# A fixed order for ScalarE's copies, turns and squares in a linear-attention layer on one Trainium2 core

## The chip, the cores and the metric

The kernel runs on one core of a Trainium2 chip. A core has five engines that work side by side and wait for each other by semaphores: TensorE (PE, matrix products into PSUM banks), VectorE (DVE, elementwise work), ScalarE (ACT, functions of one input, with a table for each kind), GpSimd (POOL) and SyncE (SP), of which the last two mostly issue DMA transfers here. The metric is the device time of one execution in microseconds; of several executions the median counts. Before the change it is 1413.25 us, the median of 3 runs (1410.88 to 1413.98).

## The reference

One input `x` of 2048 tokens by 512 channels; 16 heads of 128 channels, 4 lags. Cut to what matters:

```python
xn = layernorm(x)
q, k, v = [conv4(silu(xn @ W)) for W in (Wq, Wk, Wv)]   # causal, per channel
z, a, b = xn @ Wz, xn @ Wa, xn @ Wb
q, k = rotary(q), rotary(k)
q, k = q / max(|q|, 1e-12), k / max(|k|, 1e-12)          # per head
out = 0
for s in range(4):                                        # lag of s tokens
    attn = einsum('bshd,bshd->bsh', q, lag(k, s)) / sqrt(128)
    out += (attn * sigmoid(lag(a, s) * b))[..., None] * lag(v, s)
out = out * rsqrt(mean(out * out) + 1e-6) * norm_w * silu(z)
s = out @ Wout
g = silu((relu(xn @ sign(up).T * up_scale) @ sign(down).T) * down_scale)
return x + s * g
```

All in f32. The square of `out` (called o in the kernel) is only used for the mean over all 2048 channels, which the kernel applies at the very end, so o's squares can be added up beside the rest. The lengths of q and k don't change under the rotation, so the squares of q and k before it serve for the norms.

## The kernel before

The tokens go in 4 blocks of 512 (b = 0 to 3), the heads in 8 pairs (p = 0 to 7). A tile of a pair is 128 partitions by 2 halves by 512 tokens; each half (j = 0, 1) comes from its own PSUM bank.

`step(p, b)` is the unit. It computes q and k of pair p for block b+1, and v, z, the weighted sum o and the output projection of pair p for block b. So a stage b = -1 computes only q and k of block 0 (beside the sign network `ups`/`downs` of block 0, which fills PE), stages b = 0 to 2 do both, and a last loop does v, z and the output for block 3. The sign networks of blocks 1 to 3 follow as a tail of matmuls.

For each of q, k and v the path is the same. `project` multiplies on PE (4 matmuls a half) and ACT evicts the bank with a Silu into a "raw" tile (L330). The raw tile has 3 edge columns ahead of its 512, filled by `with_halo` (L291) from what `keep_halo` (L296) saved from the block before; after the Silus, its own last 3 columns are saved. `convolve` then takes the first product on ACT (L342, a multiplication by one weight for each half) and the three further taps for each half on DVE. The raw tiles of q and k share two buffers in turn: the raw q of the next step lies where the raw q of this step was.

k and v themselves also need edge columns, since lagged copies of them are read; they are copied by the same two helpers. `k`, `v` and `q` have one buffer each: the copy of edge columns into the next `k` waits until DVE has read the last one in its products, the one into `v` until DVE has formed the weighted terms `te`.

`turn(q)` makes the rotated copies of q: a multiplication of both halves on ACT (L371), then four operations on DVE. `products` squares q and k on ACT (L403, L404: `sq0` and `sq1`, two squares each), adds the two by a DMA (L405), multiplies q by the lagged k on DVE (`pr`) and sums `pr` by head on PE (`dots`). At the change of blocks (p = 0) the norms of q and k are taken (`norms`, a square root on ACT), inverted on DVE (`norms_in_rows`, which also saves `kept_r` on ACT, L490) and made into coefficients, which go through DRAM (`co_dram`) and come back broadcast (`bc`).

`weighted` multiplies the lagged v by `bc` on DVE into two tiles `te`, adds them to o, squares o on ACT (L554) into a spare tile and adds it to `o2_dram` by a DMA that POOL issues (in the profile `o_dram<-te` in stage 0, `o_dram<-xnT` later). In stage 0 that spare tile is the second `te`. `gated_output` makes `oz` of o, the norm's weight and z on DVE. After each odd p, `output_projection` multiplies `oz` of two pairs by the output weights (`po`), ACT copies the bank (L590) and a DMA adds it in DRAM.

Two wrappers `pe` and `dve` keep TensorE's and VectorE's instructions in the order of the program text. What goes through `nc.scalar` is placed by the scheduler; a third wrapper `act` keeps the order of the few ScalarE instructions given to it. Instructions of the same engine run in the order in which they were placed, each after its own waits, so an instruction that waits holds up all behind it. Most lines that go through a wrapper show as L76 in the profile.

Of the kernel before, what the change touches and what calls it, by code (L numbers as in the profile page):

```python
# [38 lines left out]
F32 = mybir.dt.float32  # L39
F32R = mybir.dt.float32r  # L40
AF = mybir.ActivationFunctionType
ALU = mybir.AluOpType
PSUM = bass.MemoryType.PSUM

P = 128
# [5 lines left out]
HALO = LAGS - 1  # L51
# [3 lines left out]
TB = 512  # L55
NTB = S // TB
# [25 lines left out]
def recurrent_layer(ctx: ExitStack, tc: tile.TileContext, a: dict, out: bass.AP):  # L82
# [204 lines left out]
    def with_halo(pool, name, tag, bufs, p, b):  # L287

        t = pool.tile([P, 2, HALO + TB], F32, tag=tag, name=f"{name}_{p}_{b}", bufs=bufs)

        (act if name in ("rv", "v") and p == b == 0 else nc.scalar).copy(t[:, :, 0:HALO], kept[name][:, p])  # L291
        return t

    def keep_halo(name, t, p, b):
        if b < NTB - 1:
            nc.scalar.copy(kept[name][:, p], t[:, :, TB : TB + HALO])  # L296

    def first_product(to, second_half):

# [68 lines left out]
    def turn(q):  # L368

        q0, q1 = q[:, LAGS - 1], q[:, LAGS - 2]  # L370
        nc.scalar.mul(q1, q0, turns[:, 0:1])  # L371
        for j in range(2):
            dve.scalar_tensor_tensor(
                q1[:, j, :], q0[:, 1 - j, :], turns[:, 2 - j : 3 - j], q1[:, j, :], ALU.mult, ALU.add
            )

        for s in range(2, LAGS):
            at = LAGS - 1 - s
            dve.scalar_tensor_tensor(
                q[:, at], q[:, at + 1], turns[:, 3:4], q[:, at + 2], ALU.mult, ALU.subtract  # L380
            )

    def products(p, b, q, between=None, beside_k=None):

        n = f"_{p}_{b}"
        if p or b:
            load(qks, "k", p, b)
        q0 = q[:, LAGS - 1]
        k = with_halo(qks, "k", "k", 1, p, b)
        raw = raw_of(qks, "k", p, b)  # L390
        if p == 0:
            sum_squares(p)
        convolve(1, p, raw, k[:, :, HALO:])
        keep_halo("k", k, p, b)
        if between:
            between()
        turn(q)
        if beside_k:
            beside_k()

        sq = [qks.tile([P, 2, TB], F32, tag=f"sq{j}", name=f"sq{j}" + n, bufs=3 - 2 * j) for j in range(2)]
        for j in range(2):
            nc.scalar.activation(sq[j][:, 0], q0[:, j], AF.Square)  # L403
            nc.scalar.activation(sq[j][:, 1], k[:, j, HALO:], AF.Square)  # L404
        nc.gpsimd.dma_start(sq[0], sq[1], accum_op=ALU.add)  # L405
        squares_due.append((p, sq[0]))
        def product(to, j, lo, hi):

            k0 = k[:, j, lo : lo + TB]
            k_lags = bass.AP(k0.tensor, k0.offset, [k0.ap[0], [1, hi - lo], k0.ap[1]])  # L410
            dve.tensor_tensor(to, q[:, lo:hi, j, :], k_lags, ALU.mult)

        pr = qks.tile([P, LAGS, TB], F32, tag="pr", name="pr0" + n, bufs=2)
        product(pr, 0, 0, LAGS)
        if not b or p % 2 == 0:
            pr1 = qks.tile([P, LAGS, TB], F32, tag="pr", name="pr1" + n, bufs=2)
            product(pr1, 1, 0, LAGS)
            if b:
                nc.gpsimd.dma_start(pr, pr1, accum_op=ALU.add)
            elif p < NP - 1:  # L420
                dve.tensor_tensor(pr, pr, pr1, ALU.add)
        else:

            product(q[:, :, 1], 1, 0, LAGS)
            dve.tensor_tensor(pr, pr, q[:, :, 1], ALU.add)
        if not b:

            prs = [pr, pr1] if p == NP - 1 else [pr]
            dots_due.append([p, prs, of_head[:, p], p == NP - 1, True])
            return  # L430


        for h in range(0, P, D // 2):
            first, second = slice(h, h + D // 4), slice(h + D // 4, h + D // 2)
            if p % 2 == 0:
                nc.gpsimd.dma_start(pr[first], pr[second], accum_op=ALU.add)
            else:
                both = dots_due[-1][1][0]
                nc.gpsimd.dma_start(both[second], pr[first])
                nc.gpsimd.dma_start(both[second], pr[second], accum_op=ALU.add)  # L440
        if p % 2 == 0:
            dots_due.append([p, [pr], of_heads[:, p // 2], p == NP - 2, False])
        else:
            dots_due[-1][-1] = True
# [61 lines left out]
        nc.sync.dma_start(co_dram[b].rearrange("s r t -> (s r) t"), rk)  # L506

    gated = {}

    def values(p, b, raw):  # L510

        v = with_halo(vs, "v", "v", 1, p, b)
        convolve(2, p, raw, v[:, :, HALO:])
        keep_halo("v", v, p, b)
        return v

    wos = {}
# [12 lines left out]
    def weighted(p, b, v):  # L530

        n = f"_{p}_{b}"
        parts = []
        for lo in range(0, LAGS, 2):

            bc = vs.tile([P, 2, TB], F32, tag="bc", name=f"bc{lo}" + n, bufs=3)
            for h in range(2):
                row = co_dram[b][lo : lo + 2, 2 * p + h, :]
                sp.dma_start(
                    bc[h * D // 2 : (h + 1) * D // 2], row.partition_broadcast(D // 2)  # L540
                )

            v0 = v[:, :, lo : lo + TB]
            v_lags = bass.AP(v0.tensor, v0.offset, [v0.ap[0], [1, 2], *v0.ap[1:]])
            te = vs.tile([P, 2, 2, TB], F32, tag=f"te{lo}", name=f"te{lo}" + n, bufs=1)
            dve.tensor_tensor(te, v_lags, bc.unsqueeze(2).to_broadcast([P, 2, 2, TB]), ALU.mult)
            parts.append(te)
        dve.tensor_tensor(parts[0], parts[0], parts[1], ALU.add)
        o = parts[0][:, 0]
        dve.tensor_tensor(o, o, parts[0][:, 1], ALU.add)  # L550


        o2 = xnT[:, p % 2 * 2 : p % 2 * 2 + 2, HALO : HALO + TB] if b else parts[1][:, 0]
        nc.scalar.activation(o2, o, AF.Square)  # L554
        if p == 0:
            pool.dma_start(o2_dram[b], o2)
        else:
            pool.dma_start(o2_dram[b], o2, accum_op=ALU.add)
        return o

    def gated_output(p, b, o, z):
# [58 lines left out]
    def step(p, b, beside_q=None, beside_k=None):  # L620

        at = b >= 0
        change = p == 0 and at
        q = queries(p, b + 1)
        rv = with_halo(vs, "rv", "raw", 1, p, b) if p == b == 0 else None
        if beside_q:
            beside_q()
        if change and b:
            sum_squares(p)
            norms(b)  # L630
        due = bool(dots_due) and dots_due[0][-1]
        if change and not b:

            def beside_k():
                norms(b)
                norms_in_rows(b)

        products(p, b + 1, q, (lambda: norms_in_rows(b)) if change and b else None, beside_k)
        if z_due:
            z_due.pop()()  # L640
        if at:
            load(vs, "v", p, b)
            raw = raw_of(vs, "v", p, b, 1, rv)
        if first_due:
            first_due.pop()()
        if at:
            v = values(p, b, raw)

        def strips():

            if p and p % 2 == 0:
                sum_squares(p)
            if p == NP - 2 and b + 2 < NTB:
                gate_products(b + 2)
            if p == 1 and not at:
                gate_products(0)
            if due:
                sum_dots()


        output_projections(strips if p % 2 == 0 or due else None)
        if change:
            coefficients(b)
        if at:
            load(vs, "z", p, b)
            load_wo(p, b)
            z = []
            z_of = lambda: z.append(gates_of_output(p, b))
            out_of = lambda: gated_output(p, b, weighted(p, b, v), z[0])
            if change:  # L670
                z_due.append(z_of)
                first_due.append(out_of)
            else:
                z_of()
                out_of()
        if p == (3 if at else 2):
            load_gate(b + 1)
        elif p == (4 if at else 3):
            gate()
        if b + 2 < NTB:  # L680
            if p < TC:
                statistics(b + 2, p)
            if p == TC - 1:
                centre(b + 2)
            elif p == 5:
                divide(b + 2)
# [138 lines left out]
    loads["by"] = sp  # L825
    load(vs, "v", 0, last)
    raw = raw_of(vs, "v", 0, last, 1)
    load(vs, "v", 1, last)
    load(vs, "z", 0, last)
    sum_squares(None)  # L830
# [31 lines left out]
    for p in range(NP + 1):  # L862
# [3 lines left out]
        if p:  # L866
            weights["z"] = z_weights.pop(p - 1)
            z = gates_of_output(p - 1, last)

        if p % 2 == 1 and p != 3 or p == 4:  # L870
            output_projections()
# [245 lines left out]
```

## Time and profile before

| what | value |
|---|---|
| median of 3 runs | 1413.25 us |
| the profiled execution's own time | 1409.21 us |
| its span, first to last instruction | 1407.4 us |
| mean granted TensorE clock | 0.997 |
| DVE's wait `te` on the broadcast coefficients | 16.8 us in 4 waits, longest 12.5 |
| ACT's wait for DVE before the edge columns of v (L291) | 112.1 us in 31 waits |
| ACT's wait for DVE before keeping v's columns (L296) | 78.6 us in 24 waits |
| ACT's wait for DVE before o's square (L554, `xnT`) | 58.2 us in 24 waits |
| ACT's wait for DVE before q's first square (L403) | 39.1 us in 27 waits |
| issue to landing of the DMAs of o's square | 3.8 to 13.4 us, median 8.1 |

A wait is the idle time of an engine just before an instruction, with the engine and instruction whose end released it. It costs time only where the waiting engine is the one that sets the end, or where something that this engine needs stands behind it. "L76 DVE k <- ACT k L342" reads: DVE's operation that writes k stood idle until ACT's line 342 had written k.

The busy share of each engine by stretch (start and end in us, busy time and number of instructions of PE, PEld, DVE, ACT, POOL, then granted clock, DMA share, GB/s):

```profile
0.00:200.00 200.00, 198.17 (x671) 110.10 (x672) 180.08 (x205) 127.70 (x254) 47.94 (x81) 1.00 0.79 223
200.00:340.00 140.00, 136.69 (x347) 58.42 (x346) 133.80 (x132) 66.49 (x139) 18.23 (x25) 1.00 0.81 207
340.00:630.00 290.00, 290.00 (x727) 125.03 (x726) 271.81 (x266) 133.61 (x273) 55.23 (x69) 1.00 0.86 198
630.00:860.00 230.00, 227.96 (x578) 97.46 (x577) 214.71 (x209) 105.79 (x212) 45.77 (x56) 0.99 0.81 190
860.00:1060.00 200.00, 197.97 (x494) 84.90 (x493) 182.23 (x171) 83.57 (x159) 35.25 (x43) 1.00 0.76 171
1060.00:1250.00 190.00, 189.53 (x500) 92.55 (x499) 124.89 (x116) 54.23 (x95) 34.21 (x44) 1.00 0.90 231
1250.00:1407.00 157.00, 150.79 (x653) 122.31 (x651) 84.89 (x135) 38.84 (x59) 0.00 (x0) 0.99 0.22 68
```

Stage b = -1 ends near 215 us, the stages 0, 1 and 2 near 500, 775 and 1052, the last loop near 1230.

### The profile page before, as it was taken

Reading aid. Unit: us, or ns where it says so; the run is one execution under the profiler, and the core shown is the slowest. Engines: PE = TensorE matmul, PEld = TensorE weight load, DVE = VectorE, ACT = ScalarE, POOL = GpSimd, SP = SyncE. Lnnn points to the kernel's source line nnn. Section 1 sums busy time; section 2 is a strip of 40 time slices with the busy share of each in tenths; the row PEclk is TensorE's granted clock in tenths of the full one; section 3 lists DMA queues with packets and bytes.
Section 4 is the critical chain, followed back from the end, with each engine's and each line's share of the span. In section 5 each row is a group of like instructions: output and inputs, shape, how many; then the busy total and the mean of one; then the engine's idle time right before and its main releaser. Section 6 shows DMA issues by size and latency. Waiting matters only on the chain. (4 is left out here: it accounts for less than half of the span.)

```text
span 1407.4 us, 12413 instructions
## 1 busy us (share of the span) xinstructions
PE 1391.1 (99%) x3962; PEld 690.8 (49%) x3962; DVE 1192.4 (85%) x1231; ACT 610.2 (43%) x1189; POOL 236.6 (17%) x317
## 2 busy tenths in 40 slices
PE   9999999999999999999999999999999999999998
PEld 6555544344444444444444444444434444578886
DVE  7998989999998999998999999898985997247454
ACT  7667655445444443354434533444432333232122
POOL 2222111111213121112231112020201122200000
PEclk9999999999999999999999999999999999999999
DMA  9977577889989588888977797887858989863020
GB/s 314 338 195 176 133 200 180 223 204 189 212 202 210 141 194 222 209 197 196 219 161 181 170 250 182 194 199 169 170 100 187 262 243 215 169 221 115 25 90 31
DMA packets 104985, 263.40 MB, mean 187 GB/s; under 512 B 17812, under 2 KB 18324, under 8 KB 100568
## 3 DMA queue, kind: packets, MB, share of 16 engines
q0 software_dynamic: 36672, 108.02, 39.6%
q1 hardware_dynamic: 68248, 154.58, 35.9%
q8 instruction: 32, 0.52, 0.1%
q14 instruction: 33, 0.27, 0.1%
HBM read 159.77 MB, written 52.45 MB: 151 GB/s over the span
## 5 line engine op out<-in xcount | busy, mean ns | idle before, releaser
L76 PE MATMUL po<-wo,oz 128*128 128x512 f32 x512 | 228.3, 599 | 7.4 <-DVE oz L76 7.4
L76 PE MATMUL pq<-xnT,wq 128*128 128x512 f32 (+1 forms) x528 | 226.2, 580 | 0.2 <-ACT xnT L76 0.2
L76 PE MATMUL pz<-xnT,wz 128*128 128x512 f32 x512 | 225.2, 592 | 0.5 <-ACT rv L330 0.5
L76 PE MATMUL pk<-xnT,wk 128*128 128x512 f32 x512 | 225.2, 592 | 0.0
L76 PE MATMUL pv<-xnT,wv 128*128 128x512 f32 x512 | 225.2, 592 | 0.0
L76 DVE SCALAR_TENSOR_TENSOR k<-rk,conv_w,k 128x512 f32<-128x512 f32 x192 | 142.3, 751 | 25.2 <-ACT k L342 20.6
L76 PEld LDWEIGHTS po<-wo,oz 128*128 128x128 f32 x512 | 96.5, 191 | 136.3 <-issue 109.1
L76 DVE SCALAR_TENSOR_TENSOR q<-rq,conv_w,q 128x512 f32<-128x512 f32 x192 | 141.5, 749 | 23.0 <-ACT q L342 16.2
L76 DVE TENSOR_TENSOR te<-v,bc 128x2048 f32<-128x2048 f32 x64 | 144.0, 2288 | 18.9 <-DMA bc<-co_dram 16.8
L76 PEld LDWEIGHTS pq<-xnT,wq 128*128 128x128 f32 x528 | 99.0, 189 | 123.1 <-issue 112.0
L76 PEld LDWEIGHTS pz<-xnT,wz 128*128 128x128 f32 x512 | 96.6, 189 | 124.2 <-issue 118.7
L76 PEld LDWEIGHTS pv<-xnT,wv 128*128 128x128 f32 x512 | 96.6, 189 | 123.7 <-issue 118.5
L76 PEld LDWEIGHTS pk<-xnT,wk 128*128 128x128 f32 x512 | 96.6, 189 | 120.5 <-issue 117.4
L76 DVE SCALAR_TENSOR_TENSOR v<-rv,conv_w,v 128x512 f32<-128x512 f32 x192 | 141.3, 750 | 6.9 <-ACT v L342 2.4
L76 DVE SCALAR_TENSOR_TENSOR q<-q,turns 128x1024 f32<-128x1024 f32 (+1 forms) x128 | 127.1, 1013 | 2.3
L76 DVE TENSOR_TENSOR pr<-q,k 128x2048 f32<-128x2048 f32 x52 | 117.3, 2287 | 0.9
L76 DVE CAST hid_hi<-hid 128x512 fp32r<-128x512 f32 x52 | 22.2, 427 | 92.3 <-ACT hid L732 92.3
L732 ACT ACTIVATE hid<-ph,up_scale 128x512 f32<-128x512 f32 x64 | 43.8, 685 | 109.0 <-PE ph L76 108.1
L76 PE MATMUL ph<-xs_hi,up 128*128 128x512 f32 x192 | 76.9, 400 | 0.1
L76 PE MATMUL ph<-xs_lo,up 128*128 128x512 f32 x192 | 75.7, 394 | 0.0
L76 DVE TENSOR_TENSOR te<-te,te 128x2048 f32<-128x2048 f32 x32 | 73.3, 2292 | 1.1
L405 POOL DMA_DIRECT2D sq<-sq x32 | 34.3, 1072 | 201.6 <-ACT sq L404 119.3
(148 smaller groups left out, 1678.0 us busy)
## 6 DMA issues: line engine op xcount, KB each, us to landing
bc<-co_dram SPq DMA_DIRECT2D x128, 256.0 KB
pr<-pr POOLq DMA_DIRECT2D x72, 256.0 KB, 5.7
wq<-in_wq_dram SPq DMA_DIRECT2D x32, 512.0 KB
wk<-in_wk_dram SPq DMA_DIRECT2D x32, 512.0 KB
sq<-sq POOLq DMA_DIRECT2D x32, 512.0 KB, 6.5
wv<-in_wv_dram SPq DMA_DIRECT2D x32, 512.0 KB
wz<-in_wz_dram SPq DMA_DIRECT2D x32, 512.0 KB
wo<-in_wo_dram SPq DMA_DIRECT2D x32, 512.0 KB
```

Source lines behind the costliest of these rows:

```text
L76: return self.tc.keep_in_program_order(getattr(self.engine, op)(*args, **kwargs))
L405: nc.gpsimd.dma_start(sq[0], sq[1], accum_op=ALU.add)
L732: nc.scalar.activation(hid, ph, AF.Relu, scale=scale)
```

## The change

Four things move in ScalarE's order, and all the moved instructions now go through `act`:

- The edge columns of k and v. `sum_with_halo` takes the place of `with_halo` and `keep_halo` for these two: the last columns of a tile are saved only when the next tile of the same name is made, which is after the Silus of its raw input, and the edge columns are filled then too.
- q's turn goes through `act`, in its old place in the text: behind k's convolution.
- The squares of q and k, and their DMA, come straight behind the turn, ahead of `beside_k`.
- o's square and its DMA are put into a list, `o_due`, and issued behind the next step's q (`queries`), or, in the last loop, behind the Silus of the next z.

```diff
--- before.py
+++ after.py
@@ -288,12 +288,26 @@
 
         t = pool.tile([P, 2, HALO + TB], F32, tag=tag, name=f"{name}_{p}_{b}", bufs=bufs)
 
-        (act if name in ("rv", "v") and p == b == 0 else nc.scalar).copy(t[:, :, 0:HALO], kept[name][:, p])
+        (act if name == "rv" and p == b == 0 else nc.scalar).copy(t[:, :, 0:HALO], kept[name][:, p])
         return t
 
     def keep_halo(name, t, p, b):
         if b < NTB - 1:
             nc.scalar.copy(kept[name][:, p], t[:, :, TB : TB + HALO])
+
+
+
+    to_keep = {}
+
+    def sum_with_halo(pool, name, p, b):
+
+        if name in to_keep:
+            to_keep.pop(name)()
+        t = pool.tile([P, 2, HALO + TB], F32, tag=name, name=f"{name}_{p}_{b}", bufs=1)
+        act.copy(t[:, :, 0:HALO], kept[name][:, p])
+        if b < NTB - 1:
+            to_keep[name] = lambda: act.copy(kept[name][:, p], t[:, :, TB : TB + HALO])
+        return t
 
     def first_product(to, second_half):
 
@@ -368,7 +382,7 @@
     def turn(q):
 
         q0, q1 = q[:, LAGS - 1], q[:, LAGS - 2]
-        nc.scalar.mul(q1, q0, turns[:, 0:1])
+        act.mul(q1, q0, turns[:, 0:1])
         for j in range(2):
             dve.scalar_tensor_tensor(
                 q1[:, j, :], q0[:, 1 - j, :], turns[:, 2 - j : 3 - j], q1[:, j, :], ALU.mult, ALU.add
@@ -386,24 +400,24 @@
         if p or b:
             load(qks, "k", p, b)
         q0 = q[:, LAGS - 1]
-        k = with_halo(qks, "k", "k", 1, p, b)
         raw = raw_of(qks, "k", p, b)
         if p == 0:
             sum_squares(p)
+        k = sum_with_halo(qks, "k", p, b)
         convolve(1, p, raw, k[:, :, HALO:])
-        keep_halo("k", k, p, b)
         if between:
             between()
         turn(q)
+
+        sq = [qks.tile([P, 2, TB], F32, tag=f"sq{j}", name=f"sq{j}" + n, bufs=3 - 2 * j) for j in range(2)]
+        for j in range(2):
+            act.activation(sq[j][:, 0], q0[:, j], AF.Square)
+            act.activation(sq[j][:, 1], k[:, j, HALO:], AF.Square)
+        nc.gpsimd.dma_start(sq[0], sq[1], accum_op=ALU.add)
+        squares_due.append((p, sq[0]))
         if beside_k:
             beside_k()
 
-        sq = [qks.tile([P, 2, TB], F32, tag=f"sq{j}", name=f"sq{j}" + n, bufs=3 - 2 * j) for j in range(2)]
-        for j in range(2):
-            nc.scalar.activation(sq[j][:, 0], q0[:, j], AF.Square)
-            nc.scalar.activation(sq[j][:, 1], k[:, j, HALO:], AF.Square)
-        nc.gpsimd.dma_start(sq[0], sq[1], accum_op=ALU.add)
-        squares_due.append((p, sq[0]))
         def product(to, j, lo, hi):
 
             k0 = k[:, j, lo : lo + TB]
@@ -506,12 +520,16 @@
         nc.sync.dma_start(co_dram[b].rearrange("s r t -> (s r) t"), rk)
 
     gated = {}
+    o_due = []
+
+    def squares_of_o():
+        while o_due:
+            o_due.pop(0)()
 
     def values(p, b, raw):
 
-        v = with_halo(vs, "v", "v", 1, p, b)
+        v = sum_with_halo(vs, "v", p, b)
         convolve(2, p, raw, v[:, :, HALO:])
-        keep_halo("v", v, p, b)
         return v
 
     wos = {}
@@ -551,11 +569,15 @@
 
 
         o2 = xnT[:, p % 2 * 2 : p % 2 * 2 + 2, HALO : HALO + TB] if b else parts[1][:, 0]
-        nc.scalar.activation(o2, o, AF.Square)
-        if p == 0:
-            pool.dma_start(o2_dram[b], o2)
-        else:
-            pool.dma_start(o2_dram[b], o2, accum_op=ALU.add)
+
+        def square():
+            act.activation(o2, o, AF.Square)
+            if p == 0:
+                pool.dma_start(o2_dram[b], o2)
+            else:
+                pool.dma_start(o2_dram[b], o2, accum_op=ALU.add)
+
+        o_due.append(square)
         return o
 
     def gated_output(p, b, o, z):
@@ -622,6 +644,7 @@
         at = b >= 0
         change = p == 0 and at
         q = queries(p, b + 1)
+        squares_of_o()
         rv = with_halo(vs, "rv", "raw", 1, p, b) if p == b == 0 else None
         if beside_q:
             beside_q()
@@ -825,6 +848,7 @@
     loads["by"] = sp
     load(vs, "v", 0, last)
     raw = raw_of(vs, "v", 0, last, 1)
+    squares_of_o()
     load(vs, "v", 1, last)
     load(vs, "z", 0, last)
     sum_squares(None)
@@ -866,6 +890,7 @@
         if p:
             weights["z"] = z_weights.pop(p - 1)
             z = gates_of_output(p - 1, last)
+        squares_of_o()
 
         if p % 2 == 1 and p != 3 or p == 4:
             output_projections()
```

The compiled program has the same instructions on PE and DVE in the same order as before. On ScalarE the order differs, on POOL the DMAs of o's squares come later among the others.

## The prediction

> **What bounds the kernel now.** I read the busy times first, then what TensorE (PE) waited for, then VectorE's (DVE) and ScalarE's (ACT) waits, then the timeline around each PE wait.
>
> ```profile
> PE 1391.1 (99%) x3962; PEld 690.8 (49%) x3962; DVE 1192.4 (85%) x1231; ACT 610.2 (43%) x1189; POOL 236.6 (17%) x317
> ```
>
> PE is busy for all but 16.3 of 1407.4 us. An edit of ACT's order adds and removes no matmul, so it can win only PE's waits (and the slower matmuls that follow one), and lose by new waits. These are PE's waits, with total, times and longest:
>
> ```profile
> PE po L76 <- DVE oz L76: 7.4, 3, 3.3
> PE unread L76 <- DVE still L690: 1.6, 1, 1.6
> PE pz L76 <- ACT rv L330: 0.5, 1, 0.5
> ```
>
> The three waits for oz (the gated output) are the prize. The timeline puts them at 275.07 (3.31 us, stage b=0), 845.62 (2.04, b=2) and 1056.13 (2.02, start of the last stage). The rest of the idle time is the start (1.6 + 0.2) and a tail of some 6 us after the last matmul, which holds no moved instruction. The second wait costs more than its length:
>
> ```profile
> 275.07 5.42 PE L76 MATMUL po<-wo,oz 128*128 128x512 f32 x12 [3.31 <-DVE oz L76]
> ...
> 845.62 7.11 PE L76 MATMUL po<-wo,oz 128*128 128x512 f32 x12 [2.04 <-DVE oz L76]
> ```
>
> The same twelve matmuls take 5.42 us after the first wait and 7.11 after the second: 1.7 us more, and in the stretch 845.62 to 849.50 the granted clock was 0.68 of full against 1.00 after the first wait. So the second wait is worth 2.04 + 1.7 = 3.7 us.
>
> oz comes from DVE, which in stages b=0 to 2 has little air: in the windows 340 to 630 and 630 to 860 us it is busy 272 of 290 and 215 of 230. What it waits for there is ACT:
>
> ```profile
> DVE k L76 <- ACT k L342: 20.6, 16, 1.8
> ...
> DVE q L76 <- ACT q L342: 16.2, 12, 3.6
> ```
>
> ACT is only 43% busy, so these are questions of order. Line 342 is the first multiplication of a convolution, on which DVE's three taps for each half wait. Just before the wait of 845.62, DVE and then ACT:
>
> ```profile
> 800.79 4.56 DVE L76 SCALAR_TENSOR_TENSOR q<-rq,conv_w,q 128x512 f32<-128x512 f32 x6
> 807.17 4.57 DVE L76 SCALAR_TENSOR_TENSOR k<-rk,conv_w,k 128x512 f32<-128x512 f32 x6 [1.83 <-ACT k L342]
> ```
>
> ```profile
> 805.38 1.15 ACT L371 ACTIVATE q<-q,turns 128x1024 f32<-128x1024 f32 x1 [1.12 <-DVE q L76]
> 806.43 0.71 ACT L342 ACTIVATE k<-rk,conv_w 128x512 f32<-128x512 f32 x1
> ```
>
> q's turn (L371) needs q complete, and k's first multiplication, whose input is ready at 804.3, stands behind it: DVE idles 1.83 = 1.15 + 0.71 less an overlap. From there to 845.62 DVE runs almost without a gap.
>
> **The change part by part.** Nothing is added or removed; PE's and DVE's orders are the same, ACT's changes.
>
> *Turn and squares behind k's first products.* At p=1 of b=2 the compiled order now has k's first multiplication straight behind the first Silu of raw k: the 1.83 goes to 0. In most odd steps, though, another thing stands there: the copy of the next raw q's edge columns (0.1 to 0.2) waits for DVE to end q's convolution, since the two raw slots take turns, and it lies ahead of the second Silu of raw k (0.58), behind which the kept columns (3 x 0.1) and the multiplication (0.65 to 0.71) now follow. DVE then idles 0.1 + 0.6 + 0.3 + 0.7 = about 1.8 where it idled 1.83 (p=3 of b=1, at 598.40: no change). Where the copy lies behind that Silu (p=1 of b=1, at 519.76) it is 1.2: 0.6 won.
>
> *Step p=5 of b=1.* Before, the gate's sigmoid and its two table loads (1.28 + 0.63 + 1.28) stood ahead of q's second multiplication: idle of 2.75 at 668.23 and 0.83 at 673.63. Now they stand behind both; the 1.8 of the last paragraph takes their place: 2.75 + 0.83 - 1.8 = 1.8 earlier (2.0 with the 0.25 at 663.16). *Step p=7 of b=1*: 0.84 + 1.41 + 1.41, part of it behind o's square (1.06), becomes 1.8: 1.9 earlier. *p=0 of b=2*: the copy of the norms' last columns, which waits for DVE's reciprocal, now stands ahead of q's turn: DVE waits 1.15 + 0.2 = 1.4; in return an idle of 0.46 at 771.40 goes. In sum DVE reaches the oz of 845.62 earlier by 2.0 + 1.9 - 1.4 + 0.5 + 1.8 = 4.8 us, and 2.04 was wanted: that wait goes, with its slow matmuls: **-3.7**. Bounds: 0 (none of the idle is won) to -3.7.
>
> *Last steps of b=2.* DVE's idle before the wait of 1056.13:
>
> ```profile
> 1019.46 2.33 DVE L76 SCALAR_TENSOR_TENSOR q<-rq,conv_w,q 128x512 f32<-128x512 f32 x3 [0.85 <-ACT q L342]
> 1023.09 2.33 DVE L76 SCALAR_TENSOR_TENSOR q<-rq,conv_w,q 128x512 f32<-128x512 f32 x3 [1.31 <-ACT q L342]
> 1027.25 4.57 DVE L76 SCALAR_TENSOR_TENSOR k<-rk,conv_w,k 128x512 f32<-128x512 f32 x6 [1.83 <-ACT k L342]
> ```
>
> All three go: o's square stands behind q's multiplications, the turn behind k's. 4.0 won where 2.02 is wanted: **-2.0** (bounds 0 to -2.0). The wait of 0.48 on ACT at 1111 is covered then: **-0.5**.
>
> *Edge columns of k and v kept later.* ACT waited 78.6 us for DVE's v to keep its columns and 112.1 for the v buffer, with the Silus of z and the eviction of po behind it. PE lost only the 0.48 by that, so the gain on PE is inside the sums above.
>
> *First stage (b=-1).* Its steps p=1, 2, 3, 7 also get the copy ahead of k's multiplications, where before k's first product ran early: DVE's k comes 1.2 to 2.3 us later. PE there waits for DVE's split of the hidden layer, with 0.6 to 4.4 us to spare at its four uses; at the use near 129 us, 0.63 is to spare and about 1.0 is taken: **+0.3** (bounds 0 to +1.7, the whole lateness).
>
> *o's square behind the next q, at p=0 of b=0.* The square ran at 259.29 and its DMA was issued at 260.64, landing 7.6 us later, and the second product of the next weighted sum (268.28, which waited 0.72 for that landing) writes the same buffer. Now the square stands behind the first Silu of raw k (input at 259.6): issue about 1.0 later, so the first PE wait grows: **+0.9**, beside the 0.3 of before (bounds 0 to +1.7).
>
> *o's squares in the last stage.* The last one moves from 1201 behind the Silu of z (input 1208.2), its DMA from 1204.1 to 1210, landing some 8.6 later; then the load and sum of squares, done at about 1224.7 against 1219. The RMS rows are wanted at some 1230 by PE, whose chain behind them waited 0.13 at 1252.98: **+0.3** (bounds 0 and +3, with the longest landing of these DMAs, 13.4, in place of 8.6).
>
> **Sum**: -3.7 - 2.0 - 0.5 + 0.3 + 0.9 + 0.3 = -4.7. The profiled execution took 1409.2 (span 1407.4, 1.8 around it), so it would take 1404.5. It lies 4.0 below the median of 1413.25; the runs spread from 1410.9 to 1414.0. On the median: **1408.5 us**.
>
> [...]
>
> **The rivals.**
> *R1, half clock after the first wait.* That wait grows to 4.2 us. Price, by the rows of twelve matmuls: 7.11 - 5.42 = 1.7. For: 2.04 was enough at 845. Against: 3.31 was not at 275. 1404.5 + 1.7, on the median 1410.2.
> *R2, the second gain is not won.* DVE's gains of p=5 and p=7 are taken back at the block change, where the norms' rows go through DMAs (DVE waited 16.8 us in 4 for such rows, once 12.5): then DVE comes only 1.8 - 1.4 + 0.5 = 0.9 earlier at 845.62, the wait shrinks to 1.1 with its slow matmuls. -4.7 + 1.1 + 1.7 = -1.9: 1411.3. Against: before the wait at 845.62 no such DMA wait stands.
> *R3, the moved instructions don't matter.* PE waited on ACT for 0.7 us in all; what DVE wins goes into other idle time: within 1 us of 1413.
> *R4, slower: the edge copy of the next raw q becomes DVE's bound.* Place: the odd steps of b=1, where each first tap of k comes 1.8 us after q's last. If ACT's queue gives none of the old idle back (its Silus of raw k come no earlier, as the gate's table loads still stand ahead of them), p=5 and p=7 pay 1.8 each. The output projections there have 0.53 (699.04) and 1.39 us (771.83) to spare, so it decides from a loss of 0.5 in p=5. The waits up to 845.62 then grow by 3.6, and with the +1.2 of the first stages the time is +4.8, nothing else won: 1418.0. For: the copy is ahead in ten steps, and margins are thin. Against: the 1.8 stands where 3.6 and 3.7 us of idle stood.
>
> **How the numbers follow.** Forecast 0.47, R1 0.13, R2 0.12, R3 0.08, R4 0.20. A measurement of this kernel tells some 0.2% (2.8 us) from no change. The forecast (-4.7) counts as faster, R1 (-3.0) for half faster and half no change, R2 and R3 as no change, R4 as slower. Faster 0.54, same 0.26, slower 0.20. Low end: all 7.4 of the waits for oz, 0.5 and 1.7 won with none of the losses is -9.6, which is 1403.6 on the median; the end is set just inside it, at 1404.0. High end: near R4, 1417.5. The likeliest one's own range is 1405 to 1411.
>
> **What would show it.** Right: PE's waits for oz are one, near 275, of 4 to 4.5 us; the twelve matmuls at 845 take 5.4; DVE's wait for q's multiplication falls from 16.2 to under 8; k's stays near 20. The first stage: a wait of about 0.3 near 129. Wrong: waits for oz at 699 or 772 (R4), or one left near 845 (R2); a granted clock under 1 behind the first wait (R1). The forecast also falls if ACT's copies or Silus become PE's releasers, which would mean that a PSUM bank comes free too late.

## The result, and the profile after

The changed kernel takes 1408.65 us, the median of 11 runs (1407.85 to 1413.32), where the kernel before took 1413.07 beside it (11 runs, 1410.2 to 1413.98). The ratio on record is 0.9984, with a 95% interval of 0.9976 to 0.9992: 2.2 us faster, between 1.1 and 3.4, which is half of the 4.4 us between the medians. The forecast was 1408.5. In a later series, 12 runs of the changed kernel (median 1410.56) against 29 of the one before (1411.19) gave 0.9995 [0.9984, 1.0006]. So the change is worth between nothing and some 3 us, and the agreement of the median says less than it seems to: the profiled executions below tell which of the forecast's steps held.

The profiled execution after took 1410.8 us, span 1408.9. What TensorE waited for in it (total, times, longest):

```profile
PE po L76 <- DVE oz L76: 6.2, 1, 6.2
PE unread L76 <- DVE still L713: 1.6, 1, 1.6
PE ph L76 <- ACT hid L755: 1.6, 1, 1.6
PE pz L76 <- ACT rv L344: 1.1, 1, 1.1
PE pf L76 <- DVE hid_lo L76: 0.9, 1, 0.9
```

The three waits for oz have become one. The waits near 845 and 1056 us are gone, but the first is 6.2 us where it was 3.3, and there are two new waits (pf, ph) and a longer one (pz). The timeline of TensorE at the one that is left, and of VectorE just ahead of it:

```profile
278.96 7.39 PE L76 MATMUL po<-wo,oz 128*128 128x512 f32 x12 [6.17 <-DVE oz L76]
```

```profile
266.81 2.29 DVE L76 TENSOR_TENSOR te<-v,bc 128x2048 f32<-128x2048 f32 x1
272.18 2.29 DVE L76 TENSOR_TENSOR te<-v,bc 128x2048 f32<-128x2048 f32 x1 [3.07 <-DMA o_dram<-te]
```

The twelve matmuls take 7.39 us, not 5.42: half clock now follows the first wait (the granted clock is 0.50 from 276.15 to 282.98 us, and single matmuls of po take up to 1220 ns where 592 is the median). VectorE stood 3.07 us for the landing of o's first square, 0.72 before the change. The places where time is lost, by profile (the slower matmuls are those twelve less 5.42; the second profile is that of `changed_again`, below):

| us | before | after | after, second profile | four_mended (below) |
|---|---|---|---|---|
| hidden layer's split, near 131 | 0 | 0.88 | 0.89 | 0 |
| first oz wait, near 275 | 3.31 | 6.17 | 4.61 | 2.51 |
| slower matmuls behind it | 0 | 1.97 | 2.98 | 0 |
| second oz wait and slower matmuls, near 845 | 3.73 | 0 | 0 | 0 |
| third oz wait, near 1056 | 2.02 | 0 | 0 | 0 |
| raw v, near 1097 | 0.47 | 1.07 | 1.36 | 0 |
| behind the RMS root, near 1254 | 0.13 | 1.58 | 2.03 | 1.93 |
| sum | 9.7 | 11.7 | 11.9 | 4.4 |
| the profiled execution's own time | 1409.21 | 1410.8 | 1412.84 | 1402.43 |

The sums follow the times, but in the second profile only in part: its time is 3.6 us over the one before, its sum 2.2. What the rest went into the table doesn't hold; the mean granted clock of that execution was 0.995, that of the two ahead of it in the table 0.997. The profiled executions of the changed kernel lie 2 us above its medians, the one of the kernel before some 4 below its median, so they show the places and not the verdict.

What the change was to bring, VectorE at p=1 of b=2, it brings: k's convolution follows q's without a gap, where 1.83 us stood.

```profile
804.04 4.56 DVE L76 SCALAR_TENSOR_TENSOR q<-rq,conv_w,q 128x512 f32<-128x512 f32 x6
808.51 4.56 DVE L76 SCALAR_TENSOR_TENSOR k<-rk,conv_w,k 128x512 f32<-128x512 f32 x6
```

VectorE's waits after (total, times, longest) show one line that the profile before did not have, the second:

```profile
DVE k L76 <- ACT k L356: 23.2, 16, 2.3
DVE te L76 <- ACT v L76: 16.4, 3, 12.6
...
DVE q L76 <- ACT q L356: 8.7, 5, 3.4
```

The weighted sum waits for ScalarE's copy of v's edge columns, once for 12.6 us. That is in the last stage, and matters below.

### The profile page after: what moved, and what is told of

It reads as the page before. It is cut to its first block, busy times and chain, and to the rows that moved or that the text cites. A ratio compares the mean times of both kernels' runs of the same rounds, so it can differ in the third digit from the quotient of the medians.

```text
span 1408.9 us, 12420 instructions
## 1 busy us (share of the span) xinstructions
PE 1390.8 (99%) x3962; PEld 690.6 (49%) x3962; DVE 1191.8 (85%) x1231; ACT 612.4 (43%) x1189; POOL 236.1 (17%) x317
## 4 chain that ended last, share of the span: by engine, by line
PE 83%; DVE 8%; DMA 5%; issue 1%; ACT 1%; SPq 1%; POOL 0%; DVEq 0%; ACTq 0%; POOLq 0%
PE pq L76 14%; PE pk L76 14%; PE po L76 14%; PE pz L76 13%; PE pv L76 12%; PE pf L76 7%; PE ph L76 7%; DVE te L76 2%; DVE q L76 2%; DVE k L76 1%; PE dots L76 1%; DVE v L76 1%; PE squares L76 1%; DMA y<-s_dram 1%; DMA bc<-co_dram 1%
## 5 line engine op out<-in xcount | busy, mean ns | idle before, releaser
L76 DVE SCALAR_TENSOR_TENSOR k<-rk,conv_w,k 128x512 f32<-128x512 f32 x192 | 141.7, 751 | 27.7 <-ACT k L356 23.2
L344 ACT ACTIVATE rq<-pq 128x512 f32<-128x512 f32 x62 | 37.0, 596 | 109.8 <-PE pq L76 109.6
```

What stands on the lines that cost most here:

```text
L76: return self.tc.keep_in_program_order(getattr(self.engine, op)(*args, **kwargs))
L344: nc.scalar.activation(to[:, j, :], pp, AF.Silu)
```

## The experiments

All times are medians, ratios are against the kernel before, measured in the same series of runs. The changed kernel has two ratios, 0.9984 and 0.9995, and its median differs by 1.9 us between its two series, while the expectations mostly count from the first one, 1408.65. So a time is best compared by its ratio. A "margin" is the time from the end of VectorE's first piece of a pair's oz, on which the waits above fell, to the start of the matmul that reads it, worked out from the trace, where TensorE did not wait.

**The next raw q's edge copy behind the squares** (`rq_edge_behind`). The tile is made right behind the squares, pinned there, and handed to the next step:

```diff
+        next_rq.append(with_halo(qks, "rq", "raw", 2, (p + 1) % NP, b + (p + 1) // NP))
...
-        convolve(0, p, raw_of(qks, "q", p, b), q0)
+        convolve(0, p, raw_of(qks, "q", p, b, raw=next_rq.pop() if next_rq else None), q0)
```

> The changed kernel with one thing moved: the copy of the next raw q's edge columns goes behind this step's squares of q and k, so it no longer stands ahead of k's first multiplications. Theory A (the changed kernel's k is late in the odd steps because ScalarE waits in that copy for VectorE to end q's convolution): VectorE's wait for k's multiplication falls from 23.2 us in 16 to under 12; the wait of 0.88 us at 131 us goes; the weighted sum of the first stage starts about 1.5 us earlier and the first oz wait shrinks from 6.2 us to 3 to 5; the oz margins before the old waits near 847 and 1054 grow from 2.0 and 2.2 us to over 3. Time 1 to 4 us under the changed kernel's 1408.65: 1404.5 to 1407.5. Rival B (the size of the first wait is set by when the DMA of o's first square lands, whatever VectorE does before): the first wait stays at 5 to 6.5 us, time within 1 us of 1408.65.

Measured: 1411.12 us (12 runs), 0.9993 [0.9982, 1.0003]. VectorE does come earlier: the margins near 562, 704 and 847 us grow from 1.1, 2.5 and 2.0 to 2.6, 5.2 and 3.2. But the one near 1053 stays at 2.20, and the ratio lies between those of the changed kernel. Nothing waited at these places any more. VectorE's wait for k does not fall either (24.6 us): in the step p=7, where it now waits 3.9, VectorE has caught up with TensorE, and waits for raw k itself. The wait at 131 us stays at 0.88, so there the copy isn't the cause; A falls for the first stage. The first oz wait is 4.4 us with a landing wait of 1.3 in it, which tells little, as the changed kernel's second profile has 4.6 and 1.5.

**A tile of its own for o's squares in stage 0** (`own_tile_for_square`).

```diff
-        o2 = xnT[:, p % 2 * 2 : p % 2 * 2 + 2, HALO : HALO + TB] if b else parts[1][:, 0]
+        o2 = xnT[:, p % 2 * 2 : p % 2 * 2 + 2, HALO : HALO + TB] if b else vs.tile([P, 2, TB], F32, tag="o2", name="o2" + n, bufs=1)
...
-        oz = vs.tile([P, 2, TB], F32, tag="oz", name=f"oz_{p}_{b}", bufs=3)
+        oz = vs.tile([P, 2, TB], F32, tag="oz", name=f"oz_{p}_{b}", bufs=2)
```

> The changed kernel with o's squares of stage 0 in a tile of their own (room is made by two buffers of oz in place of three), so that no product of the weighted sum waits for a DMA to land. Theory A (of the first oz wait of 6.2 us, 3.1 are the wait for the DMA of o's square and the rest is VectorE's lateness): the 3.07 us wait of VectorE for that DMA is gone, the first oz wait is 3.0 to 3.5 us, the time 2.5 to 5 us under 1408.65 (the slower matmuls behind the wait may go too). Rival B (two buffers of oz or another transfer take its place): the wait stays over 5 us, or new waits for oz appear; time within 1 us of 1408.65 or above.

Measured: 1407.96 us (12 runs), 0.9971 [0.9959, 0.9983]. The landing wait is gone and the first oz wait is 2.99 us, as A said; slower matmuls still follow it (the twelve take 7.11 us). The median is only 0.7 us under 1408.65; by the ratios the gain is 1.8 to 3.4 us, near A's lower end. The wait for raw v grew to 1.9 us and takes part of it back. The edit also takes one of oz's three buffers away. VectorE shows it at 1198.50, where oz waits 9.2 us for TensorE's output projection, but in time that it would else spend on v's edge copy, for which 0.9 us of waiting is left (more on that copy below).

**The turn and the squares free again, the rest changed** (`turn_and_squares_old`).

```diff
-        act.mul(q1, q0, turns[:, 0:1])
+        nc.scalar.mul(q1, q0, turns[:, 0:1])
...
-            act.activation(sq[j][:, 0], q0[:, j], AF.Square)
+            nc.scalar.activation(sq[j][:, 0], q0[:, j], AF.Square)
```

The squares also stand behind `beside_k` again.

> The changed kernel with q's turn and the squares of q and k back as before the change (free for the scheduler, squares behind what runs beside k); the edge columns and o's squares stay changed. Theory A (the waits near 845 and 1056 went because k's first products no longer stand behind the turn): VectorE's wait for k's multiplication rises from 23 us to over 28 with 1.8 us each at the odd steps of stage 2; the oz margins at 847 and 1054 fall from 2.0 and 2.2 us to under 1, with one of the two waits back at 0.2 to 2 us; time 1409 to 1413. Rival B (it is o's square behind q's multiplications that brought the gain): both waits stay away and the time is within 1 us of 1408.65.

Measured: 1429.81 us (4 runs), 1.0122 [1.0104, 1.014]; far beyond both theories. ScalarE at p=1 of b=1, and VectorE there:

```profile
533.00 1.15 ACT L385 ACTIVATE q<-q,turns 128x1024 f32<-128x1024 f32 x1 [1.61 <-DVE q L76]
534.05 0.58 ACT L344 ACTIVATE rk<-pk 128x512 f32<-128x512 f32 x1
...
535.47 1.33 ACT L356 ACTIVATE k<-rk,conv_w 128x512 f32<-128x512 f32 x2
```

```profile
536.22 4.56 DVE L76 SCALAR_TENSOR_TENSOR k<-rk,conv_w,k 128x512 f32<-128x512 f32 x6 [3.25 <-ACT k L356]
```

With the edge columns kept late, both of k's first products stand behind the second Silu of raw k. If the turn is free, the scheduler puts it ahead of that Silu, and k waits for turn, Silu, copies and product: 3.25 us where the kernel before had 1.83. VectorE's wait for k is 39.3 us in all (23.2 after), and oz is waited for five times, 14.7 us. The run takes back the turn and the squares together; that the turn is what costs is read from the trace.

**The edge columns as before, the rest changed** (`edge_columns_old`). `with_halo` and `keep_halo` are back for k and v.

```diff
-        k = sum_with_halo(qks, "k", p, b)
         convolve(1, p, raw, k[:, :, HALO:])
+        keep_halo("k", k, p, b)
```

> The changed kernel with the edge columns of k and v filled and kept as before the change; turn, squares and o's squares stay changed. Theory A (keeping the columns late costs in the first stage, since k's first product can no longer run ahead of the second Silu, and wins nothing on TensorE later): the wait of 0.88 us at 131 us goes, the first oz wait shrinks by 1 to 2 us, no wait near 845 or 1054; ScalarE's waits for VectorE before v's edge columns and before keeping them are back at some 100 and 70 us. Time 1405.5 to 1408. Rival B (late keeping is what frees ScalarE for the Silus and q's first products): waits for oz near 845 or 1054 come back with 1 to 2 us each; time 1410 to 1413.

Measured: 1426.74 us (4 runs), 1.0107 [1.0087, 1.0126]. Again far beyond both. VectorE's wait for k does fall, to 6.1 us, but a wait for the turn takes its place: 33.1 us in 25. ScalarE and then VectorE at p=0 of b=0:

```profile
250.56 0.20 ACT L296 COPY kept_k<-k 128x6 f32<-128x6 f32 x1 [1.57 <-DVE k L76]
250.66 1.14 ACT L76 ACTIVATE q<-q,turns 128x1024 f32<-128x1024 f32 x1
```

```profile
251.84 2.73 DVE L76 SCALAR_TENSOR_TENSOR q<-q,turns 128x512 f32<-128x512 f32 x3 [1.31 <-ACT q L76]
```

The pinned turn stands behind the instruction that was written just ahead of it on ScalarE, and with the old helper that is the copy that keeps k's last columns, which waits for VectorE to end k. So VectorE ends k, and must wait a copy and a multiplication for the turn: 1.31 us, nearly every step. The two parts of the change lean on each other: late columns need the turn behind k's products, and a pinned turn needs the columns kept late. On this reading neither has a price of its own.

**o's squares at once, the rest changed** (`o_squares_old`): `square()` in place of `o_due.append(square)`, through `nc.scalar`.

> The changed kernel with all of o's squares issued at once and free for the scheduler, as before the change; turn, squares of q and k and edge columns stay changed. Theory A (the place of o's squares gives part of the gain in the stages and part of the loss in the last one): VectorE's first products of q wait behind the square at some steps or not, the oz margins at 847 and 1054 stay over 1 us; the wait for raw v at 1097 is 0.5 or less; time 0 to 1.5 us under the changed kernel of the same call. Rival B (like the other two parts, taken back alone it costs much): new oz waits of over 3 us in all, time over 1415.

Measured: 1411.77 us (12 runs), 1.0 [0.999, 1.0011], 1.2 us over the changed kernel of the same series (1410.56), which is within what can be told. VectorE comes a little later (the margin near 847 is 0.6 in place of 2.0), the wait for raw v is gone, and the one behind the RMS root is 3.0 us. This part alone moves little.

**The last stage's squares as before** (`last_squares_old`), and **only the sign weights' loads put behind the squares** (`up_load_behind_square`).

```diff
-        o_due.append(square)
+        square() if b == NTB - 1 else o_due.append(square)
```

```diff
-            pool.dma_start(up[:, some], signs_dram["up"][:, some])
+            o_due.append(lambda: pool.dma_start(up[:, some], signs_dram["up"][:, some]))
```

> The changed kernel with o's squares of the last stage alone as before the change (at once, free for the scheduler, their DMAs ahead of the sign weights' loads on GpSimd's queue). Theory A (the late squares cost at two places of the last stage: the first load of sign weights, no longer held behind o's DMA, runs ahead of the broadcast coefficients near 1078 us, and the last square holds the output's DMAs on GpSimd's queue near 1212 to 1224 us): TensorE's wait for raw v (1.07 us at 1097) falls to 0.5 or less, though the 2 us gained ahead of it stay; the wait for the hidden layer behind the RMS root (1.58 us at 1254) falls to 0.5 or less. Time 1406 to 1407.5, that is 1 to 2.5 us under the changed kernel's 1408.65. Rival B (both waits are DMA latency that differs from run to run): they stay within 0.5 us of 1.07 and 1.58, time within 1 us of 1408.65.

> The changed kernel with the loads of the sign weights in the last stage put behind o's squares, as their order on GpSimd's queue was before the change; the squares stay late. Theory A: the broadcast of the coefficients lands before 1083 us, VectorE's wait for it falls from 15.4 us to 13 to 14, the wait for raw v at 1097 goes to 0.5 or less; the wait behind the RMS root stays at 1 to 2.9 us. Time 0.5 to 1.5 us under 1408.65. Rival B (the load doesn't matter, the broadcast lands when other transfers let it): wait of 15 us or more, wait for raw v still 1 us or more.

Measured: 1409.96 us (0.9993 [0.9982, 1.0004]) and 1409.61 us (0.9991 [0.9981, 1.0001]), 12 runs each. In both the wait for raw v is gone, and VectorE's wait for the broadcast coefficients is 13.0 and 12.0 us (15.4 after): in the changed kernel GpSimd sends 512 KB of sign weights at 1077.67, in the middle of these broadcasts, because the square whose DMA had stood ahead of that load now comes later. That part of A is shown, by the loads alone too, and all fourteen profiles agree: where the load runs ahead (eight) that wait's longest is 15.3 to 17.1 us and raw v is waited for 1.1 to 1.9, where it does not (six) 11.9 to 13.2 and 0 to 0.6. But the wait behind the RMS root grew to 2.3 and 4.7 us, so A falls there, and the time gained at raw v is paid again.

**The first stage as before** (`first_stage_old`): for block 0 of q and k, `with_halo`, `keep_halo`, the free turn and the free squares.

```diff
+        k = with_halo(qks, "k", "k", 1, p, b) if b == 0 else None
...
+        by = nc.scalar if b == 0 else act
```

> The changed kernel with the first stage (q and k of block 0) as before the change: edge columns of k, turn and squares free for the scheduler there. Theory A (what the change loses before 280 us it loses in the first stage): the wait for the split hidden layer (0.88 us at 131) goes, the first weighted sum starts 1.5 us earlier, the first oz wait is 3 to 4.5 us in place of 6.2; the waits near 845 and 1054 stay away. Time 1.5 to 3 us under 1408.65. Rival B (the old turn order costs later, or only the landing of o's first square counts): first oz wait 5 us or more, time within 1 us of 1408.65.

Measured: 1408.08 us (12 runs), 0.9975 [0.9964, 0.9986]. The wait at 131 us is gone and the first oz wait is 2.97 us; slower matmuls still follow (the twelve take 7.11). The waits for raw v (1.6) and behind the root (2.7) are longer than in the changed kernel. By the medians 0.6 us of it reaches the time, by the ratios 1.3 to 2.8, where A said 1.5 to 3.

**All of these mends at once** (`four_mended`): first stage, own tile, edge copy behind the squares from block 1 on, last stage's squares.

> All that looked like a loss undone at once: first stage as before the change, o's squares of stage 0 in a tile of their own, the next raw q's edge copy behind the squares in the later stages, o's squares of the last stage as before. Theory A (the losses are separate and add up): no wait for the hidden layer at 131, first oz wait 0.5 to 2.5 us, no others, waits in the last stage 0.5 us or less each; time 1402 to 1405. Rival B (as in the run with the edge copy moved, what is gained before the last stage becomes waiting for the coefficients there): oz waits as said, but the waits for raw v and behind the RMS root grow to 2 us or more each; time 1406 to 1409.

Measured: 1404.77 us (6 runs), 0.9964 [0.9951, 0.9978]. What TensorE waits for:

```profile
PE po L76 <- DVE oz L76: 2.5, 1, 2.5
PE ph L76 <- ACT hid L764: 1.9, 1, 1.9
PE unread L76 <- DVE still L722: 1.6, 1, 1.6
```

The losses before the last stage are separate and add up; A holds but for the root. This version and its variant below are the fastest measured; this one is 5.1 us under the kernel before by the ratio. Its interval lies below that of the changed kernel's second series and just touches that of the first, with 6 runs. That no slower matmuls follow its first wait of 2.51 us (the twelve take 5.42) may be in part chance, as 2.97 was enough in `first_stage_old` and 2.04 in the kernel before.

**Only the very last square early** (`last_square_early`), and **the same on top of the four mends** (`mended_and_last_early`): the last z's Silus are pinned, so that the square stays ahead of them.

```diff
-            nc.scalar.activation(to[:, j, :], pp, AF.Silu)
+            (act if n == "z" and p == NP - 1 and b == NTB - 1 else nc.scalar).activation(to[:, j, :], pp, AF.Silu)
```

> The changed kernel with only o's very last square ahead of the last z's Silus again (the Silus are pinned behind it). Theory A (the late square holds GpSimd's queue, so the output's last DMAs leave in a bunch, the sign weights' loads behind them start nearer to the sum of squares and their traffic delays its way through DRAM): the square's DMA is issued some 32 us before the row of sums is copied (24.5 us in the changed kernel), the loads some 4.6 us before (3.2), the RMS root starts 15.5 to 16.5 us after the copy (17.4), and TensorE's wait there is 0 to 0.7 us (1.6). Time 0.5 to 1.5 us under the changed kernel of the same call. Rival B (the delay of the root is chance): root 17 us or more after the copy, wait over 1 us.

> The kernel of four_mended with o's very last square ahead of the last z's Silus too. Theory A: TensorE's wait behind the RMS root falls from 1.9 us to 0.7 or less, the other waits stay as they were (first oz wait 2 to 3 us); time 1403 to 1404.5 against four_mended's 1404.77, 6 to 8 us under the kernel before. Rival B (chance): the wait stays near 2 us and the time near 1404.8.

Measured: 1413.48 us (12 runs), 1.0014 [1.0002, 1.0026], and 1405.63 us (6 runs), 0.9958 [0.9943, 0.9973]. The first is slower than the kernel before, and 2.9 us over the changed kernel of the same series. The order was as meant, but the square's DMA left 24.5 us before the row's copy again, and the wait behind the root is 3.5 and 4.0 us: A fell in both. The first profile also has a wait for oz of 1.61 us near 562, behind a landing wait of 2.99 at 373.92 (1.18 in the changed kernel); a margin of 1.1 us does not hold in every execution. The square is late for another reason than its place. ScalarE and VectorE of the changed kernel show it:

```profile
1201.51 0.58 ACT L612 COPY part<-po 128x512 f32<-128x512 f32 x1 [2.85 <-PE po L76]
1201.99 0.20 ACT L76 COPY v<-kept_v 128x6 f32<-128x6 f32 x1
```

```profile
1202.22 4.49 DVE L76 TENSOR_TENSOR te<-v,bc 128x2048 f32<-128x2048 f32 x2 [12.64 <-ACT v L76]
```

In the last loop `values`, which makes v, is written behind the output projection. The pinned copy of v's edge columns therefore stands behind the four copies of the output's banks, and VectorE idles 12.6 us for 0.2 us of work. Before the change the copy ran at 1183.69 and the last weighted sum started at 1193.08, 9 us earlier. What follows from it is in SyncE's queue, after and before:

```profile
1232.55 0.33 SPq L964 DMA_DIRECT2D x<-in_x_dram  x1
...
1247.43 1.99 SPq L950 DMA_DIRECT2D ss_dram<-row  x4
```

```profile
1230.96 0.33 SPq L939 DMA_DIRECT2D x<-in_x_dram  x1
...
1245.84 2.00 SPq L925 DMA_DIRECT2D ss_dram<-row  x4
```

The late square holds GpSimd's queue (its last addition of squares starts at 1223.67, before 1218.73), the output's DMAs behind it leave in a bunch, the tail's first loads start 1.6 us later, and the sums of squares go out behind those loads. In both traces the first load follows the landing of one of these DMAs, issued at 1226.59 before and 1226.76 after; it lands 4.0 us later before and 5.4 after. In all fourteen profiles the root comes 21.0 to 23.2 us after the first of these loads, whatever its distance to the row's copy (16.0 to 20.5). In all twelve with the late edge columns the weighted sum starts 34.0 us before that copy; in the two with the old ones 43.0 (before) and 46.4 (`edge_columns_old`), and these have the shortest ways from copy to root, 16.0 and 16.5. But the other twelve, with the same 34.0, lie from 17.0 to 20.5, so most of what differs there has another origin, and the gap between 16.5 and 17.0 is small. That the edge copy starts this chain is argued from these comparisons and the trace, not shown: no run moved that copy alone.

**The changed kernel again** (`changed_again`).

> The changed kernel again, as the control of this call and for a second profile of it. Theory A (its waits are places in the program, their lengths vary by a microsecond or two with DMA landings): one oz wait near 279 us of 4 to 7 us, 0.9 us for the hidden layer near 131, 1 to 2 us for raw v near 1097 and 1 to 3 us behind the RMS root; time 1408 to 1411, 1 to 4 us under the kernel before in the same call. Rival B (the gain seen first was chance): no difference within 0.1 per cent.

Measured: 1410.56 us (12 runs), 0.9995 [0.9984, 1.0006], with the waits of the table, each at its place and within A's bounds. The places are the program's, the lengths vary. The time is within A's bounds too, but it is only 0.6 us under the kernel before, where A said 1 to 4, and within B's 0.1 per cent. This series alone shows no gain.

## Why the prediction was right, and where not

*The two late oz waits: right.* Both went, in each of the two profiles. VectorE reached oz near 845 us 4.0 us earlier relative to TensorE (2.0 late before, 2.0 to spare after), against 4.8 in the working. The pieces fit: at p=1 of b=2 the idle went from 1.83 to 0; with the next q's edge copy ahead, k waits 1.99 us at 604, 675 and 745 (1.8 said) and 1.36 at 526 (1.2 said). In all, VectorE's wait for q's first products fell from 16.2 to 8.7 us, where under 8 was said, and that for k's rose to 23.2 and 24.9, where near 20 was said. Near 1053 the margin is 2.2 us in every kernel profiled but two, the one before and `turn_and_squares_old`: in the last step VectorE waits for raw q and raw k from TensorE (1.27 and 1.11 us in the changed kernel), so more can't be won there.

*"-0.5, covered then": wrong.* The wait for raw v (at 1097.56; the text's 1111 was a slip) grew to 1.07 and 1.36. VectorE's half of the chain did start 2.1 us earlier, but the coefficients go through DRAM, and the step left out that o's DMA also stood ahead of a load on GpSimd's queue. With the load put back behind it the wait was gone.

*"+0.9" for the first oz wait: right in its place, too small.* It measured +2.9 and +1.3, the wait for the landing growing from 0.72 to 3.07 and 1.5, and the 1.97 and 2.98 us of slower matmuls came on top. That is R1, half clock behind the first wait, and by the prediction's own signs it speaks against the forecast's path; R1's time, 1410.2, is 0.4 us from the median of the second series. The first stage's part was named at 0.3 and measured 0.88 at 131 us, plus some 1.5 us of lateness of the first weighted sum (257.24 against 255.71 for its addition); `first_stage_old` takes both back.

*"+0.3" for the last stage: wrong in its mechanism.* It priced the way of the last square through the sum of squares. That way is covered, as the row's copy hardly moved (1236.20 against 1236.07), and with the last stage's squares as before the wait is still 2.3 us. What measured +1.45 and +1.9 comes from SyncE's queue, where the row's way out stands behind loads that start later. The trace points to v's edge copy, pinned behind the output's copies, as the start of it, which the prediction counted at nothing; that it is the cause is not shown.

So a gain of 5.7 us was real and was read rightly, while the losses, set at 1.5 us, came to 7.8 and 8.0 in the two profiles (by the table, raw v's growth among them). By the profiles alone the change loses 2 us, so a median within 0.2 us of the forecast is luck. That the median still fell 4.4 us in the first series, against 0.6 between the medians of the later one, comes with the spread of the runs (1407.6 to 1414.7 in 23 runs of the changed kernel). Half clock is a part of it: the three runs with a granted clock of 0.998 took 1407.6 to 1408.1 us and the two with 0.995 took 1412.5 and 1412.8, but the eight with 0.996 lie anywhere from 1408.6 to 1414.7. How the rest divides stays open.

*R2 and R3* did not come about: no oz wait was left at 845, and what VectorE won did reach TensorE. *R4*'s copy is there at the price it said, 1.8 to 2.0 us, but the idle time it replaced was larger, and the waits it foresaw at 699 and 772 us did not appear (margins of 2.5 and 5.5).

## What to carry to other kernels

Fixing an engine's order by hand pins an instruction behind whatever happens to be written ahead of it: look at what that is in every stage of the program, since in the last loop it was four copies that waited for TensorE, and a 0.2 us copy cost VectorE 12.6. An edit made of parts that lean on each other can't be priced part by part: two of them taken back alone cost some 16 to 19 us each, by the ratios. And when a transfer moves later in a queue, list what now runs ahead of it; here it was a load that delayed the very data that the gain depended on.

## What the runs showed of the hardware

The slower matmuls did not go by the length of TensorE's wait alone. The twelve matmuls behind the first wait took 5.42 us after waits of 3.31, 3.76, 2.51 and 2.50 us, and 7.0 to 8.4 after 2.97, 2.99, 4.29, 4.41, 4.61, 4.93, 5.14, 5.61, 6.17 and 11.42. Of these fourteen waits none over 4 us escaped, and below that 2.97 was enough while 3.76 was not. In `turn_and_squares_old` a wait of 2.56 us left the sixteen matmuls behind it, at 1105.47, at 7.11 us, and one of 1.87 has 8.83 behind it, at 1114.45.

The granted clock in the profiles of the kernel before and of the changed one shows what it went with. Half clock stands from 846.98 to 850.39 us and from 1403.35 on before, from 276.15 to 282.98 and from 1405.96 on after, with 1.00 between. The stretches ahead of the last matmul are 3.41 us and twice 3.41 long, and in each profile the second one begins a whole number of 3.413 us behind the first (163 and 331 times). So in these two profiles the changes of the clock lie on a grid of 3.41 us, which the waits don't set: at 276.15 half clock begins in the middle of a wait that ends at 278.96. The kernel before at 845 us, in two windows of this grid, with TensorE's busy time first and the granted clock third from the end:

```profile
843.57:846.98 3.41, 1.37 (x4) 0.67 (x4) 3.27 (x5) 2.20 (x3) 0.88 (x1) 1.00 0.56 217
846.98:850.39 3.41, 3.41 (x5) 1.35 (x4) 3.30 (x5) 1.18 (x3) 0.22 (x1) 0.50 0.85 137
```

The whole wait of 2.04 us lies in the first window, and the second is at half clock. The first wait of that kernel, 3.31 us, is cut by the grid into 1.78 and 1.53, and the 2.02 us at 1056.13 into 1.08 and 0.94; both stay at full clock. In the changed kernel 3.35 of the 6.17 us of the first wait lie in one window, and half clock follows, while the 1.58 behind the RMS root stay at full clock. From 10 us to the last matmul these two windows with 2.04 and 3.35 us of idle time are the only ones of the two profiles that half clock follows from full clock, and in no other at full clock did TensorE idle more than 1.78 us. So what counted here is the part of a wait that falls into one window, and the limit lay between 1.78 and 2.04 us; the slower matmuls behind 1.87 us agree with it. From these rows, as an estimate: a wait under 1.78 us is not followed by half clock wherever it falls, and a longer one up to 4 us according to its place.
